# A cross-attention kernel: the statements of its steady round in another order

## The chip, the cores and the metric

The kernel runs on one core of a Trainium2 chip. The metric is the device time of one launch in microseconds; lower is better. In this text PE is the matmul engine (PEld its weight loads), DVE the vector engine, ACT the scalar engine, POOL the GpSimd engine, and SP the queue that issues the DMA transfers. Each of them works through a queue of its own, in the order in which the program lists its statements, and waits on semaphores for results of the others.

## The reference

64 independent batches of cross attention in float32, each with 256 rows of text (`x`, 512 wide) and 256 rows of audio (`ctx_768`, 384 wide):

```python
text_p  = einsum('bld,dh->blh', H_l, W_text)  + b_text
audio_p = einsum('bsd,dh->bsh', H_a, W_audio) + b_audio
Q = layer_norm(text_p, g1, beta1)
K = layer_norm(audio_p, g2, beta2)
V = audio_p
scores  = einsum('blh,bsh->bls', Q, K) / sqrt(512)
alpha   = softmax(scores)
H_hyper = einsum('bls,bsh->blh', alpha, V)
H_hyper = einsum('blh,hk->blk', H_hyper, W_out) + b_out
return layer_norm(H_hyper + H_l, g_out, beta_out)
```

## The kernel before, in words

One batch is one round of work, and batches are pipelined: while one batch has its scores computed, the next ones have their projections, and earlier ones their context, output product and last normalisation. The first three rounds and the last three are written out by hand. The loop `for b in range(3, B - 3)` writes the other 58; this text calls one pass through it a round. The program is scheduled by hand (`tc.manual_schedule()`): the order of the statements in the loop's body is the order of the instructions in each engine's queue.

In round `b` the names mean:

- `at` (batch b): scores and softmax. `last` (b - 1): context product. `old` (b - 2): rest of the context, then the output product `y = old.o`. `settled` (b - 3): last layer norm. `done`: the one before, which is stored.
- `q2`, `k2` (batch b + 2): projections of text and audio; `q3` (b + 3): the first product of the next text projection. `q[b+1]`, `k[b+1]`: their rows come back transposed from DRAM.

Matrix products are cut into fewer, cheaper ones of sums of blocks. Each has steps that add blocks up beforehand and steps that combine partial products in PSUM:

- `Fork` (`q2`; PE at L733, 128x256): products `seven, six, five, four, two, three`, and `one` for the next batch. Between them DVE does `start_q3`, `step_r` and `after_five`, ACT `after_seven` and `after_one`. Two PSUM banks (`ps_f`).
- `Thirds` (`k2` and `y`; PE at L557, 128x171): `one` (bank n), `two` (bank m), `three` (bank u), `four` (u, m, m, l, l), `five` (n, n, m, m, u). Between them ACT copies `n1` (L594), `t` (L605), `n`, `u`, and DVE does `start_t`, `start_l0`, `start_l1`, `take_m`, `start_u` (all through the helper at L541), and then for `k2` `leave_ends`, `middle_v`, `leave_middle`, `middle_less`, for `y` `plus_ends`, `plus_middle`, `plus_n0`, `last_10`, `last_01`, `last_11`, `last_00` (L707). Four PSUM banks m, l, u, n, which `k2` and `y` use by turns.
- scores (PE at L884, 128x128): `score_part(1, 7, 6, 5, 4, 3, 2)` with `open_scores`, `copy_p1`, `copy_p7`, `add_p7`; context (PE at L1033, 128x128): `z_part(7, 1, 6, 5)` for `last` and `(2, 4, 3)` for `old`, with `keep_z7` (L1044), `copy_z1`, `add_u3`, `add_c22`, `add_c21`; `context_two` (PE at L1095, 128x256).
- block sums on POOL: `cs[b+3].add` (seven), `x_new.add` (four), `query_step`, `key_step`, `c_step`, `e_step`, two `z_step`; the other six `z_step` are DVE's.
- transposes on DVE: `turn_c`, `turn_x`, `turn_e`, `k.turn([0])`, `k.turn([1])`, `q.turn` (L76, L520). The blocks they turn are fetched by groups of four transfers (`fetch_e`, `q2.fetch`, `k2.fetch`, `load_c`, `load_x`). For the last three batches `k.turn([0])` turns both halves, and `k.turn([1])` does nothing:

```python
if self.name == "q" or self.b >= B - 3:
    if 0 in halves:
        turn(self.T, self.sq, HC)
    return
```

- the last layer norm: `totals` (POOL), `deviation`, `last_deviation` (ACT), `shift` (L1348) and `settle` (L1357) on DVE, each over 128x512 in SBUF.

Uses of one PSUM bank by different engines follow each other in the order of the program. The order of the loop's body is therefore all that sets what waits for what around the change.

Of the kernel before, what the change touches and what calls it, by code (L numbers as in the profile page):

```python
# [9 lines left out]
F32 = mybir.dt.float32  # L10
# [5 lines left out]
P = 128  # L16
# [6 lines left out]
def kernel(  # L23
# [20 lines left out]
    B, L, D = x.shape  # L44
# [16 lines left out]
    small = ctx.enter_context(tc.tile_pool(name="small", bufs=4))  # L61
# [7 lines left out]
    def squares(dst, src):  # L69

        v = src.rearrange("(b j) (q f) -> q j b f", j=SQ, q=NQ)
        for q in (0, 2, 1, 3):
            nc.sync.dma_start(dst[q * SQ : (q + 1) * SQ], v[q])
# [7 lines left out]
    def load_c(b):  # L81
        cq = blk.tile([P, S // SQ, DA // NQ], F32, tag="cq", name=f"cq_{b}")
        squares(cq, c[b])
        blocks[b] = [cq]

    def load_x(b):
        xq = blk.tile([P, L // SQ, D // NQ], F32, tag="xq", name=f"xq_{b}")
        squares(xq, x[b])
        blocks[b].append(xq)
# [5 lines left out]
    def load_x_rows(b):  # L95
        x_rows[b] = xin.tile([P, LT, D], F32, tag="x", name=f"x_{b}")
        nc.sync.dma_start(x_rows[b], x[b].rearrange("(t p) d -> p t d", p=P))

    def load_c_rows(b):
        c_rows[b] = cin.tile([P, ST, DA], F32, tag="c", name=f"c_{b}")  # L100
        nc.sync.dma_start(c_rows[b], c[b].rearrange("(t p) d -> p t d", p=P))
# [30 lines left out]
    x_rows, c_rows = {0: x_0}, {0: c_0}  # L132
# [15 lines left out]
    ba_sb = row(b_audio, "ba")  # L148
# [386 lines left out]
    def scales_of(a, b, var):  # L535

        r = rstd_beside(var, 4)
        a.r, b.r = r[:2], r[2:]
# [851 lines left out]
    q, k, xT, cT, xs, cs, att = {}, {}, {}, {}, {}, {}, {}  # L1390
# [7 lines left out]
    done = None  # L1398
# [6 lines left out]
    pool, tag = (once, 'e')  # L1405
# [49 lines left out]
    wa_blocks = third_weights(wa_sb, wa_t, [3])  # L1455
# [14 lines left out]
    wt_blocks = weight_sums(wt_sb, DC // 2, 'wtsum')  # L1470
# [68 lines left out]
    ba_delta = third_bias(ba_sb, 'ba_delta')  # L1539
# [384 lines left out]
    q2_2.fetch()  # L1924

    for b in range(3, B - 3):
        at = att[b]
        settled, old, last = att.pop(b - 3), att[b - 2], att[b - 1]
        k2 = k[b + 2] = Thirds("k", b + 2, cs.pop(b + 2), wa_blocks, ba_sb, ba_delta)
        q2 = q[b + 2]  # L1930
        x_old = x_rows[b - 2]

        var = small.tile([P, 4], F32, tag="var4", name="var")
        old.context_two(0)
        old.z_part(2)
        old.context_two(1)
        last.fetch_e()
        old.z_part(4)
        old.z_part(3)
        old.copy_top()  # L1940
        cT[b + 3] = turn_c(b + 3)
        old.copy_two()
        q2.seven()
        at.affine_queries(0)
        k2.one()
        k2.copy_n1()
        settled.totals()
        old.add_c21()
        old.product_sums()
        y = old.o  # L1950
        old.z_step(0)
        at.affine_queries(1)
        at.query_sums()
        at.query_step(0)
        old.z_step(7)
        q2.after_seven()
        old.z_step(1)
        k2.start_t()
        q2.six()
        if b + 4 < B: load_c(b + 4)  # L1960
        at.open_scores()
        k2.two()
        settled.deviation(0)
        q2.start_q3()
        k2.three()
        at.score_part(1, 7)
        old.z_step(3)
        old.z_step(2)
        q2.step_r()
        last.context_sums()  # L1970
        last.c_step(0)
        k2.copy_t()
        q2.five()
        k2.start_l0()
        k2.start_l1()
        old.z_step(4)
        at.copy_p1()
        xT[b + 3] = turn_x(b + 3)
        k2.four()
        q2.after_five()  # L1980
        k2.take_m()
        settled.deviation(1)
        k2.start_u()
        cs[b + 3] = Sides(cT.pop(b + 3), "csum").add(0)
        cs[b + 3].add(1)
        at.affine_queries(3)
        settled.last_deviation()
        settled.shift(1)
        k[b + 1].turn([0])
        at.affine_queries(2)  # L1990
        k2.five()
        k2.copy_n()
        q2.four()
        k2.copy_u()
        k2.leave_ends()
        old.z_step(5)
        k2.middle_v()
        at.copy_p7()
        k2.leave_middle()
        q2.two()  # L2000
        y.seed()
        q2.square(var[:, :2], [1])
        k2.leave()
        at.query_step(1)
        k2.square(var[:, 2:], [0])
        k2.middle_less()
        y.one()
        settled.settle(1)
        y.copy_n1()
        at.query_step(2)  # L2010
        old.z_step(6)
        last.turn_e()
        at.score_part(6)
        at.add_p7(0)
        if b + 4 < B: load_x(b + 4)
        q2.three()
        k2.square(var[:, 2:], [1])
        q2.square(var[:, :2], [0])
        cs[b + 3].add(1)
        scales_of(q2, k2, var)  # L2020
        y.start_t()
        cs[b + 3].add(1)
        last.c_step(1)
        k[b + 1].turn([1])
        at.score_part(5)
        y.three()
        last.c_step(2)
        at.add_p7(1)
        y.copy_t()
        y.two()  # L2030
        q2.normalise([1])
        last.weight_sums()
        last.e_step(0)
        load_c_rows(b)
        last.open_context()
        last.z_part(7)
        q[b + 1].turn()
        at.query_step(3)
        x_new = SumX(xT.pop(b + 3))
        x_new.add(1)  # L2040
        y.start_l0()
        if done: done.store()
        done = settled
        at.score_part(4)
        y.start_l1()
        at.score_part(3)
        last.keep_z7()
        at.score_part(2)
        q2.normalise([0])
        last.z_part(1)  # L2050
        cs[b + 3].add(1)
        k2.normalise([1])
        last.copy_z1()
        y.four()
        settled.shift(0)
        last.e_step(1)
        at.maxima()
        k2.normalise([0])
        last.e_step(2)
        last.z_part(6)  # L2060
        x_new.add(1)
        cs[b + 3].add(1)
        y.take_m()
        Fork.seed()
        att[b + 1] = Attention(b + 1)
        att[b + 1].affine_keys(0)
        y.start_u()
        y.five()
        at.exponentials([0])
        q2.store()  # L2070
        k2.store()
        at.exponentials([1])
        last.add_u3()
        att[b + 1].affine_keys(1)
        settled.settle(0)
        x_new.add(1)
        x_new.add(1)
        y.plus_ends(x_old)
        y.plus_middle(x_old, 1)
        last.c_step(3)  # L2080
        last.z_part(5)
        q3 = q[b + 3] = Fork(b + 3, x_new.of, wt_blocks)
        q3.one()
        cs[b + 3].add(1)
        q2.fetch()
        cs[b + 3].add(1)
        att[b + 1].affine_keys(2)
        at.reciprocals()
        y.plus_n0()
        last.add_c22()  # L2090
        y.plus_middle(x_old, 0)
        att[b + 1].affine_keys(3)
        y.last_10()
        att[b + 1].key_sums()
        att[b + 1].key_step(0)
        at.divide_e([0])
        at.divide_e([1])
        att[b + 1].key_step(1)
        q3.after_one()
        y.last_01(x_old)  # L2100
        att[b + 1].key_step(2)
        y.last_11()
        at.store_e()
        k2.fetch()
        load_x_rows(b - 1)
        k2.seed()
        y.last_00()


# [128 lines left out]
    settled, old, last = (att[B - 5], att[B - 4], att[B - 3])  # L2238
# [5 lines left out]
    at = att[B - 2]  # L2244
# [232 lines left out]
```

## Time and profile before

| | |
|---|---|
| median of 3 runs | 1338.17 us (1337.62 to 1338.43) |
| the profiled execution | 1337.96 us, of which the span from first to last instruction 1336.2 us |
| busy share of the span: PE, PEld, DVE, ACT, POOL | 99%, 94%, 93%, 87%, 86% |
| DMA queue of SP | 320.20 MB, 85.8% of 16 engines' span |
| PE waits of over 0.15 us | two, 1.6 us and 0.2 us, both before the loop |
| the 58 rounds of the loop | 94.59 us to 1273.81 us of the span |

The time lies a little above the span, since it holds what is around the program's own instructions. In rows of the timeline the columns are start us, length us, engine, line, operation, output and inputs, shape, number of instructions run together, and in brackets the idle time before with what ended it. PE's matmuls appear twice as often as the program writes them. They are pipelined: a row's length runs to the modelled end of its last matmul, while the next one starts earlier; the chain of waits has the pieces without this overlap.

### The profile page before, as it was taken

What the parts mean: (1) busy time and instruction counts of PE and PEld (TensorE: products, weight loads), DVE (VectorE), ACT (ScalarE), POOL (GpSimd) and SP (SyncE); (2) the same over time, 40 slices, a digit from 0 to 9 for tenths busy, and PEclk for the clock granted to TensorE, in tenths of its full rate; (3) what the DMA queues carried; (4) which work ended last, traced back from release to release, by engine and by line L of the source; (5) the groups of instructions that cost most, each with busy time, mean ns of one, the idle gap of its engine ahead of it and who ended that gap; (6) DMA issues with size and microseconds to landing.
All of it is one profiled execution on the core that took longest, in us unless ns stands there. A gap on an engine that the chain in (4) does not pass through costs nothing.

```text
span 1336.2 us, 29969 instructions
## 1 busy us (share of the span) xinstructions
PE 1329.2 (99%) x8495; PEld 1249.4 (94%) x8495; DVE 1244.4 (93%) x3313; ACT 1163.4 (87%) x3310; POOL 1153.6 (86%) x1855
## 2 busy tenths in 40 slices
PE   9999999999999999999999999999999999999998
PEld 5889999999999999999999999999999999999996
DVE  6669999999999999999999999999999999999968
ACT  4898898898998988888988988989889889889885
POOL 5778898898898988988988988988989889889865
PEclk9999999999999999999999999999999999999999
DMA  9888889989888899888888899889888998888773
GB/s 223 222 243 230 239 252 244 250 244 253 250 246 233 257 250 239 257 246 240 251 245 248 250 244 253 246 232 261 248 234 257 252 240 253 245 243 252 210 233 135
DMA packets 448972, 322.24 MB, mean 241 GB/s; under 512 B 153765, under 2 KB 381349, under 8 KB 448806
## 3 DMA queue, kind: packets, MB, share of 16 engines
q1 hardware_dynamic: 448710, 320.20, 85.8%
q8 instruction: 68, 1.11, 0.4%
q14 instruction: 98, 0.80, 0.2%
q10 hardware_dynamic: 96, 0.13, 0.0%
HBM read 203.57 MB, written 116.65 MB: 240 GB/s over the span
## 4 chain that ended last, share of the span: by engine, by line
PE 99%; ACT 0%; DVE 0%; issue 0%; POOL 0%; ACTq 0%; DVEq 0%; POOLq 0%
PE ps_f L733 29%; PE ps_m L557 16%; PE ps_sc L884 14%; PE ps_n L557 11%; PE ps_u L557 8%; PE ps_z L1033 7%; PE ps_l L557 5%; PE ps_z L1095 5%; PE ps_sc L823 1%; PE ps_f L440 0%; PE ps_m L440 0%; PE ps_n L440 0%; PE ps_l L244 0%; PE ps_u L440 0%; PE ps_fold L244 0%; PE ps_m L244 0%
## 5 line engine op out<-in xcount | busy, mean ns | idle before, releaser
L352 POOL TENSOR_TENSOR csum<-csum,cT 128x256 f32<-128x256 f32 x310 | 195.1, 630 | 5.2
L869 POOL TENSOR_TENSOR qsum<-qT 128x256 f32<-128x256 f32 x118 | 113.0, 958 | 98.7 <-ACT qT L527 92.0
L733 PE MATMUL ps_f<-wtsum,xsum 128*128 128x256 f32 x756 | 194.1, 379 | 0.0
L527 ACT ACTIVATE qT<-qT,columns 128x256 f32<-128x256 f32 x256 | 152.7, 598 | 1.8 <-DVE qT L76 1.8
L733 PEld LDWEIGHTS ps_f<-wtsum,xsum 128*128 128x128 f32 x756 | 131.9, 191 | 11.5 <-issue 0.7
L527 ACT ACTIVATE kT<-kT,columns 128x256 f32<-128x256 f32 x256 | 141.9, 610 | 0.0
L733 PE MATMUL ps_f<-wt,xT 128*128 128x256 f32 x504 | 129.5, 379 | 0.0
L884 PE MATMUL ps_sc<-kT,qT 128*128 128x128 f32 x928 | 122.5, 275 | 0.0
L884 PEld LDWEIGHTS ps_sc<-kT,qT 128*128 128x128 f32 x928 | 114.7, 192 | 0.0
L1357 DVE SCALAR_TENSOR_TENSOR yr<-yr,rstd,beo 128x512 f32<-128x512 f32 x120 | 107.9, 899 | 0.1
L884 PE MATMUL ps_sc<-ksum,qsum 128*128 128x128 f32 x696 | 106.0, 275 | 0.0
L884 PEld LDWEIGHTS ps_sc<-ksum,qsum 128*128 128x128 f32 x696 | 97.8, 191 | 3.4 <-DVE ps_sc L541 0.4
L733 PEld LDWEIGHTS ps_f<-wt,xT 128*128 128x128 f32 x504 | 91.0, 190 | 9.7
L1348 DVE SCALAR_TENSOR_TENSOR yr<-yr,nm,go 128x512 f32<-128x512 f32 x124 | 96.8, 781 | 0.0
L488 ACT ACTIVATE kr<-kr,rstd 128x512 f32<-128x512 f32 x126 | 92.5, 737 | 0.1
L1158 ACT ACTIVATE junk<-yr,nm 128x512 f32<-128x512 f32 x124 | 90.2, 728 | 0.2
L314 POOL TENSOR_TENSOR xsum<-xT 128x256 f32<-128x256 f32 x124 | 90.4, 729 | 0.0
L794 ACT ACTIVATE junk<-ps_f 128x512 f32<-128x512 f32 x126 | 75.3, 598 | 16.8 <-PE ps_f L733 15.4
L541 DVE TENSOR_TENSOR ps_l<-ps_m,t 128x171 f32<-128x171 f32 x248 | 83.6, 337 | 6.2 <-ACT t L605 1.5
L804 ACT ACTIVATE qr<-ps_f,rstd 128x512 f32<-128x512 f32 x126 | 87.9, 700 | 0.1
L520 DVE STREAM_TRANSPOSE kT<-kq 128x512 f32<-128x512 f32 x122 | 85.4, 702 | 1.3 <-DMA kq<-kd 1.2
L1095 PE MATMUL ps_z<-eT,c 128*128 128x256 f32 x296 | 84.4, 380 | 0.0
(302 smaller groups left out, 4657.1 us busy)
## 6 DMA issues: line engine op xcount, KB each, us to landing
kd<-kr SPq DMA_DIRECT2D x64, 512.0 KB, 3.1
kq<-kd SPq DMA_DIRECT2D x256, 128.0 KB, 3.2
qd<-qr SPq DMA_DIRECT2D x64, 512.0 KB, 2.8
qq<-qd SPq DMA_DIRECT2D x256, 128.0 KB, 2.9
xq<-in_x_dram SPq DMA_DIRECT2D x252, 128.0 KB, 3.1
x<-in_x_dram SPq DMA_DIRECT2D x63, 512.0 KB, 5.5
out_dram<-yr SPq DMA_DIRECT2D x62, 512.0 KB, 5.1
cq<-in_ctx_dram SPq DMA_DIRECT2D x252, 96.0 KB, 4.1
```

The costliest lines, as they stand in the source:

```text
L314: self.engine.tensor_tensor(*step)
L352: nc.gpsimd.tensor_tensor(*step)
L488: nc.scalar.mul(row, row, self.r[t])
L527: nc.scalar.activation(self.T[:, k, :], self.T[:, k, :], AF.Identity, bias=bet[:, k : k + 1], scale=gam[:, k : k + 1],)
L557: nc.tensor.matmul(place, lhsT=self.sides.of[n], rhs=self.weights[n], start=(n == 14), stop=True, skip_group_check=True,)
L733: nc.tensor.matmul(place, lhsT=side, rhs=w, start=(n == 7 and c == 0), stop=True, skip_group_check=True,)
L869: nc.gpsimd.tensor_tensor(*self.steps[n])
L884: nc.tensor.matmul(self.place(t, m), lhsT=self.qsides[n][:, c], rhs=self.ksides[n][:, c], start=False, stop=True, skip_group_check=True,)
L1033: nc.tensor.matmul(self.zp[{1: 0, 2: 0, 4: 2}.get(n, 1)], lhsT=self.asides[n], rhs=self.bsides[n], start=(n == 7), stop=True, skip_group_c ...
L1095: nc.tensor.matmul(ps, lhsT=c_rows[self.b][:, s, bass.ts(j, P)], rhs=self.eT[:, s, :], start=start, stop=(s == ST - 1), skip_group_check=True,
L1348: nc.vector.scalar_tensor_tensor(row, row, self.nm[:, t : t + 1], go_sb, ALU.add, ALU.mult)
L1357: nc.vector.scalar_tensor_tensor(self.y[:, t, :], self.y[:, t, :], self.r[t], beo_sb, ALU.mult, ALU.add)
```

## The change

The 180 statements of the loop's body stand in another order, and nothing else changes: each statement of the old body is in the new one exactly once, and the code before and behind the loop is the same. The lines that only give names (`at =`, `k2 =`, `q3 =`, `x_new =`) move along.

The order of PE's statements, before and after:

```
before: context_two(0), z2, context_two(1), z4, z3, q2.seven, k2.one, q2.six, k2.two, k2.three, score(1,7), q2.five, k2.four,
        k2.five, q2.four, q2.two, y.one, score(6), q2.three, score(5), y.three, y.two, z7, score(4), score(3), score(2), z1, y.four, ...
after:  context_two(0), context_two(1), z2, z4, z3, k2.one, q2.seven, q2.six, k2.three, k2.two, score(1,7), k2.four, q2.five,
        k2.five, q2.four, score(6), q2.two, y.one, q2.three, score(5), y.two, y.three, score(4), z7, score(3), score(2), z1, y.four, ...
```

(z2 is `z_part(2)`; from `y.four` on: z6, `y.five`, z5, `q3.one` in both.) The order of DVE's, as far as it differs:

```
before: turn_c, add_c21, z_step 0, 7, 1, k2.start_t, open_scores, start_q3, z_step 3, step_r, k2.start_l0, k2.start_l1, z_step 4, turn_x,
        after_five, take_m, start_u, shift(1), k.turn([0]), leave_ends ... middle_less, settle(1), z_step 6, turn_e, add_p7(0), y.start_t, k.turn([1]), add_p7(1), q.turn, y.start_l0, y.start_l1, ...
after:  turn_c, add_c21, k2.start_t, z_step 0, 7, 1, open_scores, start_q3, k2.start_l0, k2.start_l1, z_step 3, step_r, turn_x,
        take_m, start_u, after_five, z_step 4, shift(1), z_step 6, leave_ends ... middle_less, settle(1), add_p7(0), k.turn([0]), turn_e, y.start_t, k.turn([1]), add_p7(1), q.turn, y.start_l1, y.start_l0, ...
end:    before plus_middle(0), last_10, last_01, last_11, last_00;  after last_10, plus_middle(0), last_11, last_01, last_00
```

ACT, POOL and SP, in excerpts of the diff:

```diff
-        at.affine_queries(0)
         k2.one()
         ...
+        at.affine_queries(1)
+        k2.copy_n1()
+        old.copy_two()
+        old.copy_top()
+        at.affine_queries(0)
         ...
-        settled.deviation(0)
-        settled.deviation(1)
-        at.affine_queries(3)
-        settled.last_deviation()
-        at.affine_queries(2)
+        at.affine_queries(3)
+        at.copy_p1()
+        at.affine_queries(2)
+        at.copy_p7()
+        settled.deviation(0)
+        settled.deviation(1)
+        settled.last_deviation()
         ...
-        q2.normalise([1]), keep_z7, q2.normalise([0]), k2.normalise([1]), copy_z1, k2.normalise([0])
+        q2.normalise([0]), keep_z7, q2.normalise([1]), k2.normalise([0]), copy_z1, ..., k2.normalise([1])
         ...
-        last.e_step(1)
-        last.e_step(2)
         ...
+        last.c_step(3)
+        last.e_step(2)
         att[b + 1].key_step(0)
         ...
-        SP: fetch_e, load_c, load_x, load_c_rows, done.store, q2.store, k2.store, q2.fetch, store_e, k2.fetch, load_x_rows
+        SP: fetch_e, load_c, load_c_rows, done.store, load_x, q2.store, load_x_rows, k2.store, store_e, q2.fetch, k2.fetch
```

(The lines with several names and those marked SP put single statements of the diff side by side.)

More of the change, by code (lines that the diff above doesn't have):

```diff
@@ L1926 @@
     for b in range(3, B - 3):
+        settled, old, last = att.pop(b - 3), att[b - 2], att[b - 1]
+        old.context_two(0)
         at = att[b]
[L1928 to L1934, printed above, removed]
+        old.context_two(1)
         old.z_part(2)
-        old.context_two(1)
@@ L1937 @@
-        last.fetch_e()
         old.z_part(4)
         old.z_part(3)
-        old.copy_top()
-        cT[b + 3] = turn_c(b + 3)
-        old.copy_two()
-        q2.seven()
-        at.affine_queries(0)
-        k2.one()
-        k2.copy_n1()
-        settled.totals()
[L1948 to L1962, printed above, removed]
-        settled.deviation(0)
-        q2.start_q3()
[L1965 to L1971, printed above, removed]
+        cT[b + 3] = turn_c(b + 3)
+        k2 = k[b + 2] = Thirds("k", b + 2, cs.pop(b + 2), wa_blocks, ba_sb, ba_delta)
+        last.context_sums()
+        at.affine_queries(1)
@@ new lines @@
+        k2.one()
+        old.add_c21()
+        last.fetch_e()
+        q2 = q[b + 2]
+        k2.copy_n1()
+        q2.seven()
+        old.product_sums()
+        k2.start_t()
+        old.copy_two()
+        old.copy_top()
+        old.z_step(0)
+        q2.six()
+        old.z_step(7)
+        old.z_step(1)
+        at.open_scores()
+        at.affine_queries(0)
+        q2.after_seven()
+        at.query_sums()
+        k2.three()
+        at.query_step(0)
+        k2.two()
+        old.z_step(2)
@@ L1972 @@
+        settled.totals()
+        q2.start_q3()
+        cs[b + 3] = Sides(cT.pop(b + 3), "csum").add(0)
+        cs[b + 3].add(1)
+        last.c_step(1)
         k2.copy_t()
-        q2.five()
+        at.affine_queries(3)
         k2.start_l0()
         k2.start_l1()
-        old.z_step(4)
+        at.score_part(1, 7)
         at.copy_p1()
+        old.z_step(3)
+        q2.step_r()
+        k2.four()
         xT[b + 3] = turn_x(b + 3)
-        k2.four()
-        q2.after_five()
+        at.affine_queries(2)
@@ L1981 @@
+        at.query_step(1)
+        at.copy_p7()
+        settled.deviation(0)
         k2.take_m()
+        q2.five()
         settled.deviation(1)
         k2.start_u()
-        cs[b + 3] = Sides(cT.pop(b + 3), "csum").add(0)
+        q2.after_five()
+        x_new = SumX(xT.pop(b + 3))
+        at.query_step(2)
+        last.open_context()
         cs[b + 3].add(1)
-        at.affine_queries(3)
-        settled.last_deviation()
+        cs[b + 3].add(1)
+        k2.five()
+        old.z_step(4)
@@ L1988 @@
         settled.shift(1)
-        k[b + 1].turn([0])
-        at.affine_queries(2)
-        k2.five()
+        if b + 4 < B: load_c(b + 4)
+        old.z_step(6)
+        var = small.tile([P, 4], F32, tag="var4", name="var")
+        last.c_step(0)
+        old.z_step(5)
+        q3 = q[b + 3] = Fork(b + 3, x_new.of, wt_blocks)
         k2.copy_n()
-        q2.four()
         k2.copy_u()
         k2.leave_ends()
-        old.z_step(5)
+        x_new.add(1)
+        x_old = x_rows[b - 2]
         k2.middle_v()
-        at.copy_p7()
+        settled.last_deviation()
@@ L1999 @@
         k2.leave_middle()
+        q2.four()
+        at.score_part(6)
+        k2.middle_less()
         q2.two()
+        settled.settle(1)
+        load_c_rows(b)
+        y = old.o
+        y.one()
         y.seed()
+        at.add_p7(0)
         q2.square(var[:, :2], [1])
         k2.leave()
-        at.query_step(1)
         k2.square(var[:, 2:], [0])
-        k2.middle_less()
-        y.one()
-        settled.settle(1)
+        k[b + 1].turn([0])
         y.copy_n1()
-        at.query_step(2)
@@ L2011 @@
-        old.z_step(6)
         last.turn_e()
-        at.score_part(6)
-        at.add_p7(0)
-        if b + 4 < B: load_x(b + 4)
+        last.weight_sums()
         q2.three()
+        at.score_part(5)
+        last.c_step(2)
         k2.square(var[:, 2:], [1])
         q2.square(var[:, :2], [0])
-        cs[b + 3].add(1)
-        scales_of(q2, k2, var)
         y.start_t()
-        cs[b + 3].add(1)
-        last.c_step(1)
+        y.two()
+        at.query_step(3)
+        y.three()
         k[b + 1].turn([1])
-        at.score_part(5)
@@ L2026 @@
-        y.three()
-        last.c_step(2)
         at.add_p7(1)
[L2029 to L2032, printed above, removed]
         last.e_step(0)
-        load_c_rows(b)
-        last.open_context()
+        at.score_part(4)
         last.z_part(7)
         q[b + 1].turn()
-        at.query_step(3)
-        x_new = SumX(xT.pop(b + 3))
-        x_new.add(1)
[L2041 to L2050, printed above, removed]
-        cs[b + 3].add(1)
[L2052 to L2055, printed above, removed]
-        last.e_step(1)
-        at.maxima()
-        k2.normalise([0])
-        last.e_step(2)
[L2060 to L2070, printed above, removed]
-        k2.store()
[L2072 to L2086, printed above, removed]
@@ L2087 @@
-        att[b + 1].affine_keys(2)
-        at.reciprocals()
+        at.score_part(3)
+        scales_of(q2, k2, var)
+        y.copy_t()
+        at.score_part(2)
+        att[b + 1] = Attention(b + 1)
+        y.start_l1()
+        cs[b + 3].add(1)
+        q2.normalise([0])
+        last.keep_z7()
+        q2.normalise([1])
+        cs[b + 3].add(1)
+        if done: done.store()
+        y.start_l0()
+        last.z_part(1)
+        k2.normalise([0])
+        settled.shift(0)
+        x_new.add(1)
@@ new lines @@
+        last.e_step(1)
+        y.four()
+        if b + 4 < B: load_x(b + 4)
+        at.maxima()
+        y.take_m()
+        y.start_u()
+        last.copy_z1()
+        att[b + 1].affine_keys(0)
+        at.exponentials([0])
+        Fork.seed()
+        k2.normalise([1])
+        x_new.add(1)
+        last.z_part(6)
+        last.add_u3()
+        q2.store()
+        y.five()
+        at.exponentials([1])
+        settled.settle(0)
+        att[b + 1].affine_keys(2)
+        att[b + 1].affine_keys(3)
@@ L2089 @@
+        y.plus_ends(x_old)
+        att[b + 1].affine_keys(1)
+        last.z_part(5)
+        y.plus_middle(x_old, 1)
+        load_x_rows(b - 1)
+        at.reciprocals()
+        q3.one()
+        at.divide_e([0])
+        cs[b + 3].add(1)
+        k2.store()
         y.plus_n0()
         last.add_c22()
+        cs[b + 3].add(1)
+        at.divide_e([1])
+        q3.after_one()
+        y.last_10()
         y.plus_middle(x_old, 0)
-        att[b + 1].affine_keys(3)
-        y.last_10()
         att[b + 1].key_sums()
+        x_new.add(1)
@@ L2095 @@
+        at.store_e()
+        last.c_step(3)
+        q2.fetch()
+        last.e_step(2)
         att[b + 1].key_step(0)
-        at.divide_e([0])
-        at.divide_e([1])
+        done = settled
+        y.last_11()
         att[b + 1].key_step(1)
-        q3.after_one()
         y.last_01(x_old)
+        k2.seed()
+        k2.fetch()
         att[b + 1].key_step(2)
[L2102 to L2106, printed above, removed]
         y.last_00()
```

## The prediction

> **What bounds the kernel now.** I read the page's engine shares first, then the busy time of single rounds, then the chain inside one round, then who waits for whom around the moved statements.
>
> ```profile
> PE 1329.2 (99%) x8495; PEld 1249.4 (94%) x8495; DVE 1244.4 (93%) x3313; ACT 1163.4 (87%) x3310; POOL 1153.6 (86%) x1855
> PE 99%; ACT 0%; DVE 0%; issue 0%; POOL 0%; ACTq 0%; DVEq 0%; POOLq 0%
> ```
> PE holds 99% of the chain that ended last. A busy PE can still be a slowed PE, so single rounds have to be looked at. The four stretches below are the second and a middle one of the 58 rounds, then the first and the last (columns: length, then busy us of PE, PEld, DVE, ACT, POOL, and the granted clock):
>
> ```profile
> core 0: us, PE busy (x) PEld busy (x) DVE busy (x) ACT busy (x) POOL busy (x), PEclk, DMA share, GB/s
> 115.51:135.80 20.29, 20.29 (x135) 19.47 (x134) 19.59 (x54) 18.09 (x53) 18.13 (x30) 1.00 0.86 248
> 704.12:724.41 20.29, 20.29 (x135) 19.47 (x134) 19.58 (x54) 18.09 (x53) 18.11 (x30) 1.00 0.85 244
> 94.59:115.51 20.92, 20.89 (x137) 19.41 (x136) 20.17 (x57) 18.63 (x54) 17.90 (x29) 1.00 0.73 217
> 1252.13:1273.81 21.68, 21.61 (x139) 20.07 (x138) 20.41 (x57) 19.18 (x56) 19.27 (x32) 1.00 0.66 204
> ```
> A middle round takes 20.30 us, PE is busy in all of it, and its clock is full. Whether that is PE's own pace shows in the pieces of the chain inside one round, all of them PE's:
>
> ```profile
> 706.68 0.58 PE ps_n L557 x4
> 708.99 0.89 PE ps_sc L884 x8
> 713.65 1.73 PE ps_f L733 x8
> ```
> One matmul of 256 columns takes 1.73/8 = 0.216 us, one of 171 takes 0.58/4 = 0.145, one of 128 takes 0.89/8 = 0.111. A round has 32, 60 and 42 of them: 6.92 + 8.70 + 4.68 = 20.30. So the round is the sum of its matmuls at their own pace and holds no stall. The other four engines have 0.7 us (DVE) to 2.2 us (ACT, POOL) of idle time in it.
>
> **The change part by part.** The same statements stand in both orders, none added or removed, so each engine keeps its instructions and their durations. What can differ is waiting. In 56 of 58 rounds there is none to remove, so the middle rounds can only stay at 20.30 or grow. Loss exists in two rounds: the first (20.92 - 20.30 = 0.62) and the last (21.68 - 20.30 - 0.86 for four matmuls of the end that fall into the stretch = 0.52).
>
> *First round.* Its rows:
>
> ```profile
> 94.59 0.60 PE L1095 MATMUL ps_z<-eT,c 128*128 128x256 f32 x2
> 94.88 0.28 DVE L541 TENSOR_TENSOR zT<-ps_z,z 128x128 f32<-128x128 f32 x1
> 95.22 0.49 PE L1033 MATMUL ps_z<-eT,c 128*128 128x128 f32 x2
> 95.68 0.51 DVE L707 SCALAR_TENSOR_TENSOR yr<-ps_n,n 128x342 f32<-128x342 f32 x1
> 99.09 0.34 DVE L541 TENSOR_TENSOR ps_u<-ps_n,n 128x171 f32<-128x171 f32 x1
> 99.48 0.56 PE L557 MATMUL ps_u<-wa_thirds,csum 128*128 128x171 f32 x2
> ```
> `old.z_part(2)` is due at 94.59 + 0.43 = 95.02, but `add_c22` ends at 95.16, so it starts at 95.22, and its pair takes 0.49 where 0.39 is usual. This gives the price of lateness: PE starts 0.06 after the late result and loses another 0.10. **An input has to be ready some 0.16 us ahead.** `k2.three()` is late in the same way behind `start_t` (99.43 to 99.48). In the new order `z_part(2)` follows both `context_two`, at 95.45: in time. `k2.start_t()` moves up behind `add_c21`, about 1 us earlier: in time. But `k2.one()` now stands ahead of `q2.seven()`, due at 94.59 + 0.86 + 0.67 = 96.12, and waits for `last_11` (bank n), which ends at 96.19: it loses 0.07 + 0.06 + 0.10 = 0.23. `open_scores`, last of the same seven DVE statements, stays close to its reader: 0 to 0.35, I take 0.15. So 0.38 in place of 0.62: **-0.24** (bounds -0.6 and +0.3).
>
> *Last round.*
>
> ```profile
> 712.94 0.70 DVE L520 STREAM_TRANSPOSE kT<-kq 128x512 f32<-128x512 f32 x1
> 1260.95 1.24 DVE L76 STREAM_TRANSPOSE kT<-kq 128x1024 f32<-128x1024 f32 x1
> 1263.45 0.82 PE ps_n L557 x4
> ```
> There `k.turn([0])` turns both halves at once (1.24 for 0.70) and `turn([1])` does nothing. The 0.54 delays `leave_ends` to `middle_less`, and with them `y.one()` (0.82 for 0.58) and `score_part(5)`. In the new order the turn stands behind `middle_less`, `settle(1)` and `add_p7(0)`; ahead of the next DVE statement that PE reads soon (`add_p7(1)`) stands the empty `turn([1])`, which gives 0.70 back. `y.start_t` gets 0.54 later; `y.three()` now follows `y.two()`, which adds 0.58 of cover. So **-0.50** (bounds -0.52 and +0.3).
>
> *Middle rounds, ACT and DVE against PE.* `k2.four()` passes `q2.five()`, which takes 0.86 us of cover from `start_l0` and `start_l1`.
>
> ```profile
> 707.96 0.74 PE L557 MATMUL ps_m<-wa,csum 128*128 128x171 f32 x4
> 708.54 0.45 PE L557 MATMUL ps_u<-wa_thirds,csum 128*128 128x171 f32 x2
> 709.03 0.30 ACT L605 COPY t<-ps_u 128x171 f32<-128x171 f32 x1
> 709.36 0.72 DVE L541 TENSOR_TENSOR ps_l<-ps_m,t 128x171 f32<-128x171 f32 x2
> 710.87 0.74 PE L557 MATMUL ps_m<-wa_thirds,csum 128*128 128x171 f32 x4
> ```
> Before, `start_l1` ends at 710.08 and its reader starts at 710.87: 0.79 of room. In the new order, counted from the start of `k2.three()`: that reader is due after 0.29 + 0.58 (`k2.two()`) + 0.89 (scores) + 0.29 = 2.05. The path to it: `k2.two()`, whose bank `start_l0` reads, ends at 0.29 + 0.74 = 1.03, then 0.04 and 0.72: 1.79. The path by `copy_t` (0.45 + 0.04 + 0.30 + 0.04 + 0.72 = 1.55) is shorter. **Room 0.26**, over the 0.16 needed.
>
> ```profile
> 717.75 0.30 DVE L541 TENSOR_TENSOR ps_sc<-ps_sc,sc 128x128 f32<-128x128 f32 x1
> 718.52 0.28 ACT L605 COPY t<-ps_u 128x171 f32<-128x171 f32 x1
> 718.64 1.50 PE L884 MATMUL ps_sc<-kT,qT 128*128 128x128 f32 x12
> 719.29 0.27 ACT L1044 COPY z<-ps_z 128x128 f32<-128x128 f32 x1
> 719.98 0.39 PE L1033 MATMUL ps_z<-eT,c 128*128 128x128 f32 x2
> ```
> `score_part(4)` passes `z_part(7)` (0.22): the room behind `add_p7(1)` falls from 718.64 - 718.05 = 0.59 to 0.37. `keep_z7` waits on ACT behind `y.copy_t`, and `y.three()` moves behind `y.two()`: from its start, 0.45 (as `k2.three()`) + 0.04 to `copy_t`, then as in the rows 719.56 - 718.52 = 1.04, so 1.53, against 0.29 + 0.45 + 0.22 + 0.89 = 1.85 to `z_part(1)`: room 0.32.
>
> `k2.one()` passes `q2.seven()` and is due 0.86 earlier, at 704.12 + 1.53 = 705.65. It waits for the last reader of bank n:
>
> ```profile
> 705.11 0.51 DVE L707 SCALAR_TENSOR_TENSOR yr<-ps_n,n 128x342 f32<-128x342 f32 x1
> ```
> At its old place `last_11` ends at 705.62, too late by 0.13. But it changes places with `last_01`, whose issue takes 0.44: it ends at 705.18, room 0.47. All other inputs keep their room or gain: `k2.five()` gains 0.86 behind `start_u`, `q2.five()` 1.45 behind `step_r`, `y.one()` 0.45 behind `middle_less`, `score_part(5)` over 0.9 behind the earlier `add_p7(0)`. On ACT, `affine_queries` and `copy_p7` come earlier, `deviation`, `last_deviation` and one `normalise` slip into ACT's waits; the latter's readers are DVE's `settle` and a store, not PE. On POOL the order of the sums changes most, and `e_step(2)` goes from the middle to the end, straight ahead of `key_step(0)`:
>
> ```profile
> 724.97 1.28 POOL L866 TENSOR_TENSOR ksum<-kT 128x512 f32<-128x512 f32 x1
> ```
> Even if POOL had nothing to spare, `e_step(2)` would end there, and its reader `z_part(4)` is due at 724.41 + 0.86 + 0.22 = 725.49: room 0.5. Sum of the middle rounds: **0**.
>
> *SP.* `q2.fetch` goes behind `store_e`, `load_x_rows` ahead of `k2.store`. So eight fetch transfers lie ahead of `fetch_e`, in place of four and the row load: 1.0 MB either way.
>
> ```profile
> qq<-qd SPq DMA_DIRECT2D x256, 128.0 KB, 2.9
> eq<-ed SPq DMA_DIRECT2D x244, 64.0 KB, 4.9
> 707.74 0.88 SPq L97 DMA_DIRECT2D x<-in_x_dram  x1
> 708.72 1.90 SPq L73 DMA_DIRECT2D eq<-ed  x4
> 715.77 0.70 DVE L76 STREAM_TRANSPOSE eT<-eq 128x512 f32<-128x512 f32 x1
> ```
> (two views, transfers and timeline). The last of the four `fetch_e` is issued at 708.72 + 1.42 = 710.1 and lands about 4.9 later, 715.0, for `turn_e` at 715.77. In the new order `turn_e` stands one `turn` (0.70) later, less a `z_step` (0.2) that has left its place: 716.3. The issue comes 1.0 later (one more group of four, 1.9, less the row load's 0.9), at 711.1, and lands between 2.9 (as the fetches ahead of it) and 4.9 after that: 714.0 to 716.0. I take it as hidden; the upper bound leaves 0.3.
>
> **Sum.** Against the profiled execution (1337.96 us, span 1336.2): -0.24 - 0.50 + 0 = -0.7, 1337.2. The median is 0.21 above it: **1337.4 us**.
>
> **The rivals.**
> 1. *PE has headroom (faster).* If the time in which PEld is idle, 1336.2 - 1249.4 = 86.8 us, could be closed by another order, the time would fall to 1251 us at best. The Trainium skill (Perfetto Trace Analysis, Identifying the Most-Contended Engine) says that matmul busy time misjudges PE and that the busy share of weight loads is to be taken. By that rule the trace's 94% would be headroom; the trace does not bear it out, as follows. PEld misses 20.29 - 19.47 = 0.82 us in a round; a weight load takes 0.191, so the 32 wide matmuls of 0.216 leave 32 x 0.025 = 0.80. That idle time belongs to the matmul's width, and no order removes it. 2%.
>
> ```profile
> L733 PEld LDWEIGHTS ps_f<-wtsum,xsum 128*128 128x128 f32 x756 | 131.9, 191 | 11.5 <-issue 0.7
> ```
> 2. *The shortened cover fails (slower).* `k2.four()` catches `start_l1`. It decides from 0.26 - 0.16 = 0.10 us of delay on DVE or ACT ahead of `start_l0`. If DVE comes 0.3 late in each round, PE loses 0.20 + 0.10 at 57 rounds, 17 us: 1354. For it: DVE has only 0.7 us idle a round. Against it: DVE waits for `k2.two()` just there, so small delays vanish. 5%.
> 3. *DVE meets POOL (slower).*
>
> ```profile
> 712.28 0.74 DVE L1348 SCALAR_TENSOR_TENSOR yr<-yr,nm,go 128x512 f32<-128x512 f32 x1
> 712.43 1.19 POOL L869 TENSOR_TENSOR qsum<-qT 128x256 f32<-128x256 f32 x1 [1.58 <-ACT qT L527]
> 713.69 0.73 POOL L869 TENSOR_TENSOR qsum<-qsum,qT 128x256 f32<-128x256 f32 x1
> ```
> Of two POOL statements of one size the first starts under DVE's `shift` and takes 1.19, the second 0.73: one engine holds the other up. Four `shift` and `settle` a round now meet other POOL work; each can lose 0 to 0.73. DVE becomes the bound when the sum exceeds its 0.7 of idle time by more than the old order already pays; 2 x 0.73 - 0.7 = 0.8 us a round, 1381. The Trainium skill (SBUF — State Buffer, Who interferes with whom) states it as a lock: a DVE instruction with two SBUF inputs and a POOL instruction that reads SBUF block each other wholly; the row agrees, and the rule alone does not say which statements meet. 2%.
> 4. *`fetch_e` lands late (slower)*: it decides 0.3 beyond the upper bound above; each 0.2 more, passed on by `turn_e` to the short room of `score_part(4)`, makes 0.2 x 57 = 11 us, 1349. 3%.
> 5. *Nothing is gained at the ends:* 1338.2. Inside my range.
>
> **How the numbers follow.** 0.2% is 2.7 us, about what a measurement can tell. My forecast and rival 5: 88%, within 0.2%. Rivals 2 to 4: 10%, slower. Rival 1: 2%, faster. Range: low 1338.17 - 1.14 - 0.55 (spread of the runs) = 1336.5; high 1338.17 + 0.3 + 0.3 (upper bounds of the two end rounds) + 0.5 (handover to the end, as much as the last round lost before) + 0.26 = 1339.5. It leaves the slower rivals out, 1 in 10.
>
> **What would show it.** Middle rounds at 20.30 us with PE busy throughout; the first about 20.7; the last near 21.2; `copy_t`, two `start_l`, then the bank-m product some 0.26 later. Wrong if a middle round exceeds 20.30: then PE's pair at `k2.four()`, `score_part(4)` or `z_part(1)` starts late.

## The result, and the profile after

The new order is slower: 1357.62 us (median of 4 runs, 1357.36 to 1358.32) against 1338.30 for the old one beside it, a ratio of 1.0141 (95% interval 1.0123 to 1.0158). The forecast was 1337.4 us, no change. The profiled execution of the new order has a span of 1355.8 us, 19.6 more than before.

The stretches of the changed kernel (columns as in the prediction), a middle round, then the first and the last:

```profile
714.21:734.83 20.62, 20.54 (x136) 19.48 (x134) 19.18 (x54) 18.29 (x53) 18.35 (x29) 1.00 0.89 247
...
94.66:115.81 21.15, 20.77 (x136) 19.55 (x135) 19.66 (x57) 18.57 (x54) 18.73 (x30) 1.00 0.76 212
1270.85:1292.34 21.49, 21.40 (x140) 20.24 (x139) 20.18 (x57) 19.16 (x55) 18.73 (x30) 1.00 0.69 207
```

A middle round now takes 20.62 us in place of 20.30, at full clock. The 56 rounds between the first and the last take 1270.85 - 115.81 = 1155.04 us, before 1252.13 - 115.51 = 1136.62: 18.42 more. The first round takes 0.23 more, the last 0.19 less, and the first starts 0.07 later. The rest is 1.07 after the last round, and it lies behind the issue of the last store (L1334, at 1351.43 and, before, at 1332.91), which stands at the same distance from the last round in both (59.09 and 59.10 us). So the middle rounds are the case. The engine shares and the chain on the page of after:

```profile
PE 1341.9 (99%) x8495; PEld 1249.1 (92%) x8495; DVE 1221.7 (90%) x3313; ACT 1173.7 (87%) x3310; POOL 1167.7 (86%) x1855
...
PE 95%; ACT 2%; DVE 1%; issue 1%; SPq 1%; DMA 0%; DVEq 0%; ACTq 0%
...
L884 PEld LDWEIGHTS ps_sc<-kT,qT 128*128 128x128 f32 x928 | 119.1, 191 | 18.9 <-ACT t L605 17.2
```

PE's share of the chain falls from 99% to 95%. The last row is where PE now stands still: the weight loads of the scores' products (L884) have 18.9 us of idle time ahead of them, and the row names ACT's `t` (L605, `copy_t`) as the releaser of 17.2 of it. That name turned out to be wrong. The timeline of one middle round of after, from 714.21:

```profile
716.01 0.97 DVE L76 STREAM_TRANSPOSE cT<-cq 128x768 f32<-128x768 f32 x1
...
716.72 0.38 ACT L1114 COPY zT<-ps_z 128x256 f32<-128x256 f32 x1
...
716.91 0.25 DVE L541 TENSOR_TENSOR zT<-ps_z,u 128x128 f32<-128x128 f32 x1
717.09 0.33 DVE L541 TENSOR_TENSOR ps_u<-ps_n,n 128x171 f32<-128x171 f32 x1
717.20 0.37 ACT L1060 COPY zT<-ps_z 128x256 f32<-128x256 f32 x1
...
717.67 0.62 DVE L1084 TENSOR_TENSOR zsum<-ps_z,zT 128x256 f32<-128x256 f32 x2 [0.25 <-POOL kT L866]
...
718.21 0.41 DVE L1084 TENSOR_TENSOR zsum<-zsum,ps_z 128x256 f32<-128x256 f32 x1
718.34 0.74 PE L557 MATMUL ps_m<-wa,csum 128*128 128x171 f32 x4
718.54 0.30 ACT L605 COPY t<-ps_u 128x171 f32<-128x171 f32 x1 [0.21 <-PE ps_u L557]
...
718.75 0.27 DVE L874 MEMSET ps_sc<- 128x256 f32 x1
718.93 0.37 DVE L541 TENSOR_TENSOR ps_f<-ps_f,s 128x256 f32<-128x256 f32 x1
719.14 0.52 PEld L884 LDWEIGHTS ps_sc<-kT,qT 128*128 128x128 f32 x4 [0.31 <-ACT t L605]
719.17 0.68 PE L884 MATMUL ps_sc<-kT,qT 128*128 128x128 f32 x4
```

The same work in a middle round of before, from 704.12:

```profile
705.79 0.97 DVE L76 STREAM_TRANSPOSE cT<-cq 128x768 f32<-128x768 f32 x1
705.85 0.37 ACT L1060 COPY zT<-ps_z 128x256 f32<-128x256 f32 x1
...
706.69 0.25 DVE L541 TENSOR_TENSOR zT<-ps_z,u 128x128 f32<-128x128 f32 x1
707.08 0.62 DVE L1084 TENSOR_TENSOR zsum<-ps_z,zT 128x256 f32<-128x256 f32 x2
707.62 0.41 DVE L1084 TENSOR_TENSOR zsum<-zsum,ps_z 128x256 f32<-128x256 f32 x1
707.94 0.34 DVE L541 TENSOR_TENSOR ps_u<-ps_n,n 128x171 f32<-128x171 f32 x1
708.28 0.27 DVE L874 MEMSET ps_sc<- 128x256 f32 x1
...
708.68 0.56 PEld L884 LDWEIGHTS ps_sc<-kT,qT 128*128 128x128 f32 x4
...
708.83 0.61 PE L884 MATMUL ps_sc<-kT,qT 128*128 128x128 f32 x4
```

Read them from the bottom. `score_part(1)` is due when `k2.two()` has passed, at 718.34 + 4 x 0.145 = 718.92, and starts at 719.17: 0.25 late. Its products then take 0.68 in place of 0.61, another 0.07. Together that is the 0.32 by which the round is longer. In both orders its weight load starts 0.12 to 0.13 after the end of the memset of `open_scores` (719.02 to 719.14; 708.55 to 708.68). Counted from the round's start, the memset ends at 4.81 in place of 4.43: 0.38 late. In the old order the load stood 0.15 ahead of its product, in the new one 0.03, so the old order had 0.12 of room, and 0.38 - 0.12 = 0.26 is what PE lost.

The 0.38 comes from the DVE queue above. `turn_c` starts 0.13 later: `last_00` now stands right behind `last_01` and starts 0.04 after its end (715.75 against 715.71), where it started 0.08 before the end of `last_11` (705.54 against 705.62); why, no run shows. `copy_top` (L1060), which was done before `add_c21` (`zT<-ps_z,u`), now starts 0.04 after its end, and the first `z_step` (L1084) starts 0.10 after the end of `copy_top`: DVE stands idle for 0.25 there (the row names POOL's `kT` as the releaser; the first experiment rules that out). The memset clears the tile of the scores, which takes over the buffer of `old`'s `ps_z1`: the pool `p_at` has two buffers (kernel.py, L64), and three tiles a round take them in turn. So it has to wait for the `z_step`s that read `ps_z1`. `start_t` had kept it apart from `z_step(1)`; now it follows that one and starts 0.13 after its end; `start_t` itself stands ahead of the memset in both orders. In the old order the first `z_step` stood as directly behind `add_c21` and lost 0.14; that is gone: 0.13 + 0.25 + 0.13 - 0.14 = 0.37.

### The profile page after: what moved, and what is told of

Its sections match the earlier page's. It is cut to its first block, busy times and chain, and to the rows that moved or that the text cites. A ratio compares the mean times of both kernels' runs of the same rounds, so it can differ in the third digit from the quotient of the medians.

```text
span 1355.8 us, 29907 instructions
## 1 busy us (share of the span) xinstructions
PE 1341.9 (99%) x8495; PEld 1249.1 (92%) x8495; DVE 1221.7 (90%) x3313; ACT 1173.7 (87%) x3310; POOL 1167.7 (86%) x1855
## 4 chain that ended last, share of the span: by engine, by line
PE 95%; ACT 2%; DVE 1%; issue 1%; SPq 1%; DMA 0%; DVEq 0%; ACTq 0%
PE ps_f L733 27%; PE ps_m L557 15%; PE ps_sc L884 14%; PE ps_n L557 10%; PE ps_u L557 8%; PE ps_z L1033 6%; PE ps_l L557 5%; PE ps_z L1095 4%; PE ps_sc L823 1%; SPq L73 0%; PE ps_f L440 0%; DVE yr L707 0%; PE ps_n L440 0%; PE ps_l L244 0%; DMA c<-in_ctx_dram 0%
## 5 line engine op out<-in xcount | busy, mean ns | idle before, releaser
L733 PE MATMUL ps_f<-wtsum,xsum 128*128 128x256 f32 x756 | 184.5, 379 | 0.0
L527 ACT ACTIVATE qT<-qT,columns 128x256 f32<-128x256 f32 x256 | 154.4, 605 | 1.8 <-DVE qT L76 1.8
L733 PEld LDWEIGHTS ps_f<-wtsum,xsum 128*128 128x128 f32 x756 | 137.9, 190 | 15.0 <-issue 0.8
L527 ACT ACTIVATE kT<-kT,columns 128x256 f32<-128x256 f32 x256 | 141.9, 611 | 0.1
L884 PE MATMUL ps_sc<-kT,qT 128*128 128x128 f32 x928 | 136.1, 279 | 5.5 <-ACT qT L527 1.0
L884 PEld LDWEIGHTS ps_sc<-kT,qT 128*128 128x128 f32 x928 | 119.1, 191 | 18.9 <-ACT t L605 17.2
L866 POOL TENSOR_TENSOR ksum<-kT 128x512 f32<-128x512 f32 x59 | 75.6, 1281 | 65.3 <-ACT kT L527 65.3
L869 POOL TENSOR_TENSOR qsum<-qT 128x256 f32<-128x256 f32 x118 | 86.3, 731 | 50.8 <-ACT qT L527 50.6
L314 POOL TENSOR_TENSOR xsum<-xT 128x256 f32<-128x256 f32 x124 | 118.8, 958 | 0.0
L884 PEld LDWEIGHTS ps_sc<-ksum,qsum 128*128 128x128 f32 x696 | 100.6, 191 | 6.0
L884 PE MATMUL ps_sc<-ksum,qsum 128*128 128x128 f32 x696 | 105.8, 275 | 0.0
L1357 DVE SCALAR_TENSOR_TENSOR yr<-yr,rstd,beo 128x512 f32<-128x512 f32 x120 | 94.9, 791 | 0.1
L733 PEld LDWEIGHTS ps_f<-wt,xT 128*128 128x128 f32 x504 | 86.6, 191 | 6.7
L460 ACT ACTIVATE junk<-kr 128x512 f32<-128x512 f32 x126 | 79.6, 632 | 2.2
```

The lines of the kernel that those rows point to most:

```text
L314: self.engine.tensor_tensor(*step)
L527: nc.scalar.activation(self.T[:, k, :], self.T[:, k, :], AF.Identity, bias=bet[:, k : k + 1], scale=gam[:, k : k + 1],)
L733: nc.tensor.matmul(place, lhsT=side, rhs=w, start=(n == 7 and c == 0), stop=True, skip_group_check=True,)
L869: nc.gpsimd.tensor_tensor(*self.steps[n])
L884: nc.tensor.matmul(self.place(t, m), lhsT=self.qsides[n][:, c], rhs=self.ksides[n][:, c], start=False, stop=True, skip_group_check=True,)
L1357: nc.vector.scalar_tensor_tensor(self.y[:, t, :], self.y[:, t, :], self.r[t], beo_sb, ALU.mult, ALU.add)
```

## The experiments

The theory T: `copy_top` moved behind `add_c21`, the chain `add_c21`, `copy_top`, `z_step(0)`, memset got longer, and `score_part(1)` waits for the memset. Rivals for this last wait: R1, it waits for `copy_t`, as the trace's row says; R2, it waits for `affine_queries(0)`, which the new order put behind four other ACT statements.

**1. The new order, `copy_top` ahead of `add_c21`**

```diff
+        old.copy_top()
         old.add_c21()
         ...
         old.copy_two()
-        old.copy_top()
```

> The new order with one statement moved: copy_top stands directly ahead of add_c21, so DVE's sum waits for ACT's copy and not the copy for the sum. Theory T (copy_top now waits for add_c21, z_step(0) waits for copy_top, the memset of open_scores waits for the z_steps, score_part(1) waits for the memset): z_step(0) then waits for copy_two, which ends about 3.15 after the round's start, so it starts at 3.25 in place of 3.46; the memset ends about 0.21 earlier, and the stall of 0.245 + 0.072 at score_part(1) shrinks to 0.05 to 0.14 a round: 1341 to 1346 us. Rival R1 (score_part(1) waits for copy_t, the instruction that the trace names as its releaser): copy_t does not move, 1357.6. Rival R2 (it waits for affine_queries(0), which the new order put later on ACT): that does not move either, 1357.6.

Measured: 1343.21 us, ratio to the old order 1.0038 (1.0024 to 1.0052). A middle round takes 20.38. Its timeline, from 706.96:

```profile
709.26 0.37 ACT L1060 COPY zT<-ps_z 128x256 f32<-128x256 f32 x1
...
709.64 0.73 POOL L866 TENSOR_TENSOR kT<-kT,ksum 128x256 f32<-128x256 f32 x1
...
709.70 0.39 ACT L1114 COPY zT<-ps_z 128x256 f32<-128x256 f32 x1
...
709.97 0.63 ACT L527 ACTIVATE qT<-qT,columns 128x256 f32<-128x256 f32 x1
710.18 0.62 DVE L1084 TENSOR_TENSOR zsum<-ps_z,zT 128x256 f32<-128x256 f32 x2
...
711.26 0.27 DVE L874 MEMSET ps_sc<- 128x256 f32 x1
711.29 0.30 ACT L605 COPY t<-ps_u 128x171 f32<-128x171 f32 x1 [0.44 <-PE ps_u L557]
...
711.64 0.52 PEld L884 LDWEIGHTS ps_sc<-kT,qT 128*128 128x128 f32 x4
```

One statement gives back 14 of the 19 us. `copy_t` stands at 4.33 of the round as in the new order (711.29 - 706.96; 718.54 - 714.21), yet the load moved from 4.93 to 4.68: R1 falls, and the load still follows the memset by 0.11. The first `z_step` follows `copy_two` (L1114, ends at 710.09) by 0.09, as T says. It starts before POOL's `kT` ends (710.37), so it cannot have waited for that.

**2. The new order, both copies ahead of the affine**

```diff
         last.context_sums()
-        at.affine_queries(1)
+        old.copy_top()
+        old.copy_two()
         k2.one()
         ...
         k2.copy_n1()
+        at.affine_queries(1)
         ...
-        old.copy_two()
-        old.copy_top()
```

> The new order with copy_top and copy_two directly behind context_sums and affine_queries(1) behind copy_n1: on ACT both copies come ahead of the affine and end by 2.65 after the round's start. T: z_step(0) waits only for DVE's own start_t and starts at 3.13 to 3.21 (3.46 in the new order); the memset ends at 4.48 to 4.56, and score_part(1) is at most 0.05 late: 1337.4 if not at all, up to 1345 with the price of a late start. R1 and R2: copy_t and affine_queries(0) end within 0.05 us of where they did, 1357.6.

Measured: 1339.21 us, ratio 1.0007 (0.9998 to 1.0015). Two views of it, a middle round and the last one, and the timeline from 704.81:

```profile
704.81:725.11 20.30, 20.30 (x136) 19.47 (x135) 19.18 (x54) 18.16 (x53) 18.36 (x29) 1.00 0.94 249
...
1252.82:1273.98 21.16, 21.16 (x140) 20.23 (x138) 20.16 (x57) 19.01 (x55) 18.75 (x30) 1.00 0.67 201
```

```profile
707.32 1.12 ACT L527 ACTIVATE qT<-qT,columns 128x256 f32<-128x256 f32 x2
...
708.99 0.27 DVE L874 MEMSET ps_sc<- 128x256 f32 x1
...
709.14 0.30 ACT L605 COPY t<-ps_u 128x171 f32<-128x171 f32 x1 [0.44 <-PE ps_u L557]
...
709.38 0.56 PEld L884 LDWEIGHTS ps_sc<-kT,qT 128*128 128x128 f32 x4
...
709.79 0.72 DVE L541 TENSOR_TENSOR ps_l<-ps_m,t 128x171 f32<-128x171 f32 x2 [0.26 <-PE ps_m L557]
...
710.70 0.74 PE L557 MATMUL ps_m<-wa_thirds,csum 128*128 128x171 f32 x4
```

The middle round is back at 20.30, with every other statement where the new order has it. The load starts at 709.38, before `copy_t` ends (709.44): it cannot have waited for it. R2 falls too. `affine_queries(0)`, the last of the two L527 here, ends at the same time in both experiments (710.60 - 706.96 = 3.64 and 708.44 - 704.81 = 3.63; it did move, against my expectation, since it stands behind the copy that had waited), while the load went from 4.68 to 4.57; it ends some 1 us ahead of the load in each.

The last round is 0.52 shorter than in the old order, and the first takes 20.80, 0.12 less. This does not reach the time: the span of 1337.5 us is 1.3 above the old one's. The first round starts 0.37 later, the 56 rounds between take 0.44 more, and 1.13 lies behind the issue of the last store. From there to the end of the span it is 4.0 to 4.8 us in the changed kernel and in the first, second, fourth and last experiment, all in the new order, and 3.3 in the three kernels in the old order; no run shows why.

**3. The old order, `copy_top` behind `add_c21`**

```diff
-        old.copy_top()
         ...
         at.affine_queries(0)
+        old.add_c21()
+        old.copy_top()
         ...
-        old.add_c21()
```

> The old order with one part of the change: copy_top stands behind add_c21, both directly behind affine_queries(0). T: copy_top waits for add_c21 (ends 2.83) and ends at 3.24, z_step(0) starts at 3.34 in place of 2.96, the memset ends 0.38 later, and score_part(1) loses 0.38 - 0.13 of room + 0.07 = 0.32 a round; start_t, which stands behind the z_steps in the old order, makes k2.three late too, up to 0.1 more: 1356 to 1363 us. R1, R2: copy_t and affine_queries(0) keep their places on ACT, 1338.3, or little above for the waits of ACT.

Measured: 1358.00 us, ratio 1.0148 (1.0134 to 1.0162). The timeline from 714.79:

```profile
717.65 0.37 ACT L1060 COPY zT<-ps_z 128x256 f32<-128x256 f32 x1 [0.29 <-DVE zT L541]
...
718.12 0.62 DVE L1084 TENSOR_TENSOR zsum<-ps_z,zT 128x256 f32<-128x256 f32 x2 [0.51 <-ACT zT L1060]
...
718.99 0.34 DVE L541 TENSOR_TENSOR ps_u<-ps_n,n 128x171 f32<-128x171 f32 x1
...
719.45 0.30 PEld L557 LDWEIGHTS ps_u<-wa_thirds,csum 128*128 128x128 f32 x2 [0.33 <-issue]
719.48 0.53 PE L557 MATMUL ps_u<-wa_thirds,csum 128*128 128x171 f32 x2
```

The reversal alone makes the old order as slow as the new one, and here the two waits bear their names: the copy waits for DVE's `zT`, the first `z_step` for ACT's copy. The size is as expected, the place is not: the first PE pair to come late is `k2.three()`, behind `start_t`, 0.12 after its end; the scores behind it then lose nothing more. In the old order `start_t` stands between the `z_step`s and the memset, so the same delay meets that reader first.

**4. The new order, `copy_t` later**

```diff
-        k2.copy_t()
         at.affine_queries(3)
+        k2.copy_t()
```

> The new order with copy_t behind affine_queries(3) on ACT: copy_t ends some 0.3 later. R1 (score_part(1) waits for copy_t, as the row of its weight load says): the stall grows by about 0.3 a round, 1374 us. T: score_part(1) starts as before; start_l0, which does wait for copy_t, stands behind after_seven on DVE until 5.00 and copy_t would end at about 4.92, so nothing else is late either: 1357.6, at most 1363 if start_l0 slips by the 0.1.

Measured: 1358.29 us, ratio 1.0149 (1.0133 to 1.0164). The timeline from 714.68:

```profile
719.20 0.29 ACT L605 COPY t<-ps_u 128x171 f32<-128x171 f32 x1
719.22 0.27 DVE L874 MEMSET ps_sc<- 128x256 f32 x1
...
719.61 0.52 PEld L884 LDWEIGHTS ps_sc<-kT,qT 128*128 128x128 f32 x4 [0.31 <-ACT t L605]
```

`copy_t` came only 0.19 later, not 0.3, since ACT had idled ahead of it; it ends with the memset, at 719.49. The load stands at 4.93 of the round as before. That alone would only bound R1; with the second experiment it is out. The row still names it.

**5. The old order, memset issued twice**

```diff
         at.open_scores()
+        nc.vector.memset(at.sc[:, :, P:], 0.0)
```

> The old order with the memset of open_scores issued twice in each steady round: does the old order have room at this place? T: the old memset ends at 4.44 after the round's start, the weight load of score_part(1) follows at 4.56 and its product at 4.71; in the new order the load runs 0.03 ahead of the product, so the room is 0.12. If the second memset holds DVE for 0.18 (as one does ahead of the next statement), score_part(1) loses 0.06 + 0.07 a round: 1345 us; if it waits 0.13 for the first to end, it holds DVE for 0.40 and the loss is 0.28 + 0.07: 1358. Rival R3 (the place has the 0.3 to 0.5 of room that the prediction found elsewhere, and DVE's 0.7 of idle time takes the rest): 1338.4.

Measured: 1359.00 us, ratio 1.0156 (1.0139 to 1.0173). Its timeline, DVE and the scores' load, in the round from 714.89:

```profile
719.05 0.27 DVE L874 MEMSET ps_sc<- 128x256 f32 x1
...
719.45 0.27 DVE L1962 MEMSET ps_sc<- 128x256 f32 x1
...
719.63 0.37 DVE L541 TENSOR_TENSOR ps_f<-ps_f,s 128x256 f32<-128x256 f32 x1
...
719.84 0.52 PEld L884 LDWEIGHTS ps_sc<-kT,qT 128*128 128x128 f32 x4 [0.34 <-ACT junk L1158]
```

The second memset ends 0.40 after the first, and PE loses 0.34 a round (20.64 in place of 20.30), at `score_part(1)` alone; 0.40 - 0.12 + 0.07 gives 0.35. So the old order had 0.12 of room here, R3 falls, and DVE's 0.7 us of idle time a round covers nothing of a delay that comes just ahead of a reader. The trace now names a third releaser, ACT's `junk`.

**6. and 7. The fetch earlier, on top of the second experiment**

To look for a version that beats both, `q2.fetch()` went back behind `q3.one()`.

```diff
         q3.one()
+        q2.fetch()
         ...
-        q2.fetch()
         last.e_step(2)
```

> The best candidate: the new order with copy_top and copy_two directly behind context_sums, affine_queries(1) behind copy_n1, and q2.fetch back at its old place behind q3.one, ahead of store_e. T: middle rounds at 20.30, the last round 0.5 shorter than in the old order, the first 0.1 shorter; what is left above the old order lies in the transfers: 1337.5 to 1339.2 us, not to be told from the old order. R1 and R2: 1357.6.

Measured: 1369.04 us, ratio 1.0231 (1.0209 to 1.0254), far outside what was expected. In the old order `k2.store` stands ahead of that place, in the new one behind it. SP takes its statements in turn, so the fetch, which waits for `q2.store` to land, held back `k2.store` (`kd<-kr`) and all that follows. SP's part of a slow round, from 260.71, and DVE's row behind it:

```profile
263.35 1.81 SPq L73 DMA_DIRECT2D qq<-qd  x4
265.27 0.39 SPq L498 DMA_DIRECT2D kd<-kr  x1
...
270.48 1.88 SPq L73 DMA_DIRECT2D eq<-ed  x4
```

```profile
274.06 0.72 DVE L76 STREAM_TRANSPOSE eT<-eq 128x512 f32<-128x512 f32 x1 [0.62 <-DMA eq<-ed]
```

The fetch of `e` is issued 9.77 after the round's start; in the second experiment's kernel it is 5.65 (710.46 - 704.81). `turn_e` waits for it: over the launch DVE waits 21.3 us for `eq` in 33 places, and 5.9 us for `kq`, the fetch behind `k2.store`, in 12. With the fetch directly behind `k2.store`:

```diff
         k2.store()
+        q2.fetch()
         ...
-        q2.fetch()
         last.e_step(2)
```

> As the kernel with q2.fetch at its old place, which lost 31 us because there it stood ahead of k2.store on SP and held that store and store_e back; now q2.fetch stands directly behind k2.store, still ahead of store_e. T: PE has no stall in a middle round, as in the run with both copies first: 1337.5 to 1339.2 us. Rival: the wait of q2.fetch for the landing of q2.store still holds back store_e, and fetch_e and turn_e with it: 1345 to 1369 us.

Measured: 1338.84 us, ratio 1.0001 (0.9992 to 1.0010). No version was found that beats the old order by an amount that can be told from no change.

## Why the prediction was wrong, step by step

- **Middle rounds, "the sum: 0".** This step failed, at the sentence "All other inputs keep their room or gain". The rooms worked out were those of statements that moved against PE. The pair `open_scores` and `score_part(1)` was looked at in the first round only, although the prediction said there that it was close. Its room in every round could be read in the trace of before: load 0.13 behind the memset, 0.15 ahead of the product. It was 0.12, the memset came 0.38 later, and the 0.32 a round that this costs makes 18 over 56 rounds. The sign of being wrong that the prediction gave, a middle round above 20.30, came true, but at none of the three pairs that it named.
- **On ACT.** The prediction listed which copies come earlier or later, but not that `copy_top` passes `add_c21`. The two share no element of `zT`; both read the tile `ps_z1` in PSUM. The rule on uses of one PSUM bank, which stands ahead of the prediction, was not applied to this pair. The rows show ACT's copy waiting for DVE's sum ahead of it (it starts 0.04 after its end), and DVE's first `z_step` for ACT's copy ahead of it (0.10 after). In the old order the copy had ended 0.47 before the sum started (706.22 and 706.69), so no wait of the sum for the copy can be seen. The shared `zT` is not the reason: `copy_two` writes `zT` too but reads another tile, stands behind `add_c21` in the new order, and starts 0.19 before it (716.72 and 716.91). The Trainium skill (PSUM — Partial Sum Buffer, PSUM bank collisions raise a hardware error) says that no two engines may touch one bank in the same partitions at once, two reads included, and that the compiler's scheduler adds a dependency between them. The order of the rows here agrees with it; no run here shows the error itself.
- **`affine_queries` "come earlier".** Number 0 came later in fact. It cost nothing, as the second experiment shows.
- **First round, 0.62 to 0.38.** Measured 0.85 (21.15 - 20.30). The part at `k2.one()` was right: 0.24 for 0.23. The part of `open_scores` was taken as 0.15 with a bound of 0.35, and was about 0.61, by the same chain.
- **Last round, -0.50.** The round itself was right: with the stall gone, in the second experiment, it takes 21.16, which is 20.30 and the 0.86 of the four products of the end; the old loss has vanished. In the new order the new stall of 0.32 comes on top: 21.49.
- **The other rooms.** They held: in the second experiment's kernel no pair of a middle round is late. `start_l1` ends at 710.51 and its reader starts at 710.70, a room of 0.19 where 0.26 was worked out.
- **The price of lateness.** The form was right, the numbers nearly: the load follows its input by 0.12, the product the load by 0.03, and 0.07 is lost after it at the scores (0.06 and 0.10 had been read in the first round).
- **The rivals.** Rival 2 had the right kind and size, a cover on DVE that fails in each round by 0.2 + 0.1, 1354 us; it stood at `k2.four()`, and got 5%. Rival 3 went the other way: DVE is busy for 1221.7 us in place of 1244.4, and since PE waits for single results and not for DVE's sum, this bought nothing. Rival 4 did not come about: the new order has no wait of `turn_e` for its transfer. The sixth experiment has such waits, with some for `kq`, and takes 30 us more than the second's kernel.

## What to carry to other kernels

When statements change places around a bounding engine, take the room of every input of that engine, in the round that repeats, and begin with those whose weight load already follows its releaser by the bare handover: they have no more room than the load's lead over its product (0.12 us here), however idle the other engines are. A statement that moves past another one which reads the same PSUM tile on another engine turns the wait between them round; look for such pairs as for data. And where a row names the releaser of a wait with several inputs, compare the ends: the true one is followed at the bare handover in every kernel.

## What the runs showed of the hardware

Most DVE instructions that need nothing of the one ahead start about 0.09 us before that one ends (718.93 against 719.02). The memset starts 0.13 after the end of the `z_step` whose input it overwrites (718.75 against 718.62), and 0.13 after the end of an equal memset (719.45 against 719.32). So waiting for such a neighbour costs 0.22 us more: 0.40 from memset to memset, 0.18 from memset to the next statement. This is not one price for all: the memset behind `start_t` in the old order starts just as that ends (708.28), and `start_u`, which reads what `take_m` has just written, starts 0.03 after its end (721.84 against 721.81 in the new order). What sets these differences no run shows. The Trainium skill (VectorE: DVE Perf Modes, The DRAIN you can't avoid) says that a semaphore behind each instruction costs nothing extra, since the pipeline empties anyway, though it adds that an instruction that is not held starts earlier. For this kernel the measurement decides: behind the memset the wait costs 0.22.
